# Counting the first signs in 128 columns, and finished rows one a step in two stages

## The chip, the cores and the metric

The kernel runs on one core of a Trainium2 chip. Its engines are TensorE (PE, matrix products and transposes), VectorE (DVE), ScalarE (ACT), GpSimd (POOL) and SyncE (SP, which here only issues transfers). Each works through its own list of instructions and waits for the others by semaphores. The metric is the device time of one execution in microseconds; the lower, the better.

## The reference

Two graph layers follow each other, on 4096 nodes with 512 features. `adj` is a dense 4096 x 4096 matrix in which about one entry in 128 is above zero and the others are zero.

```python
# layer 0
head = (adj > 0) / max(sqrt(number of positive entries in the row), 1e-12)
inc = adj + head
x = layernorm(x + (inc @ x) / rowsum(inc))
# layer 1
A2 = adj + I
dscale = diagonal(A2) ** -0.5
temp = A2 @ x @ W.T
y = relu((dscale[:, None] * A2 * dscale[None, :]) @ temp)
out = layernorm(x + y)
```

So there are three products of a 4096 x 4096 matrix with a 4096 x 512 one, a small product with W, and two layer normalisations over 512 features.

## The kernel before

**Tiling.** Matrices are cut into blocks of 128 rows (`P`); there are 32 of them (`NB`), 16 in each half (`NP`). Large products are done with a scheme of seven products for eight on two by two blocks (Strassen's, in Winograd's form), which is why there are sums and differences of operands (`add_up`, `build`, `sum_b`) and combinations of results (`combine`, `outer`). The adjacency matrix comes three times: transposed in chunks for layer 0 (`adj_q`), natural by rows for counting (`adj`), and transposed in the order of layer 1 (`adj_r`).

**The start.** Layer 0 treats its first pair of row blocks (block 0 of the upper and of the lower half) apart, since nothing has been counted yet. Chunks c = 0 to 3 (`NC`) hold these rows transposed, in an upper half (h = 0) and a lower half (h = 1). SP issues, in this order: the four upper halves (`load_half(0, c)`), the rows of x for steps kk = 0 to 9 (`load_x`, two transfers of 256 KB each), the four lower halves, x for kk = 10 to 15, and then natural rows (`load_natural`, five buffers). `count_half` counts the positive entries of a row: ACT makes signs (+1 or -1) in bfloat16 in one of two `sr` buffers (`signs`, L347), and PE multiplies them by a matrix of ones (L358), which adds over the partitions and leaves the sum on every partition; `idle_products` (L363) are products whose result nobody reads. `scale_half` adds the four blocks of 128 columns that are left (L367, DVE), takes the root (L351, ACT), a lower bound and the reciprocal (L369, L370, DVE). `upper_inc` (L459, L471, L472) then makes the upper half of `inc` out of the chunk, and `multiply_plain(0, c, top)` (L510) multiplies it, four steps kk for each chunk; each step needs x of that kk. The lower half is counted between steps of `multiply_plain(0, 2, top)`; then `to_inc` (L459, L466) makes its `inc` and `multiply_plain(1, c, low)` multiplies it. Between these, DVE makes the operands of the later scheme (`build`, `build_last`) and sums that are stored for layer 1 (`raw_sums`, L440, in the same `sr` buffers, stored by POOL at L449); ACT counts natural rows (`count`, sixteen at a time, L347), each count giving a buffer free for the next natural load on SP. The next chunk (`load_chunk(NC)`, L323) stands behind these on SP. When it is there, `prepare1` readies it, and the large products of layer 0 begin (`multiply1`, L497).

**Layer 1.** `steps` lists two passes: k = 2 (A2 times x, then by W) and k = 3 (A2 times that). Each has two halves of columns s = 0 and 1, in each seven products p, and for each p a group of eight steps kk. For k = 3 the order of p is 2, 3, 5, 1, 6, 7, 4. One step is seven products (`multiply2`, L293), which PE runs as 14 matmuls of 512 columns, into seven banks of PSUM; an eighth bank (`spare`) is for everything else. `prepare` makes the sums of operands two steps ahead (L168, L170, L171, DVE). At the end of a group's last step, kk = 7, `outer` takes the seven banks into C: ACT copies q1 (L712) and q5 (L715), DVE does the rest (`inner`, L713 to L720, with an addition into C, L723 or L727, where p is 6, 7 or 4). The next group starts with the bank of q1.

**Rows that are finished.** After p = 6 the upper half of C is complete for that s, after p = 4 the lower half. Eight row units per half are then put in `queue` (the last half as four pairs, `layer1_first`). A unit, `layer1`, turns 128 rows back by four transposes into the spare bank (`turn_back`, L868), after the step's matmuls, or ahead of the fourth product where a second unit is taken (`between`); ACT scales and rectifies them into one of four buffers `o` (`rectify`, L872). In the next step its `rest` adds the residual y (three buffers, fetched by POOL, L885), takes mean and variance (L150, L152), the root (ACT, L154), the reciprocal (DVE, L160), the normalisation (ACT, L163), and stores (POOL, L901). One unit is taken a step in kk = 1 to 5; in the last two groups two a step in kk = 1 to 6:

```python
end = n >= len(steps) - 2 * NQ
items = [queue.pop(0) for _ in range(min(len(queue), 2 if end else 1))] if 1 <= kk <= (6 if end else 5) else []
```

The order inside a step is the order of the program text: `prepare` of the step after next, `sum_b`, what was `deferred` from `outer`, the products with what stands `between`, the units taken, the `rest` of the step before (`held`), `fetch`, and at kk = 7 `outer`. The last four steps are prepared like the others but multiplied product by product in `finish` (L946), with the last rows.

Of the kernel before, what the change touches and what calls it, by code (L numbers as in the profile page):

```python
# [8 lines left out]
F32 = mybir.dt.float32  # L9
BF16 = mybir.dt.bfloat16  # L10
AF = mybir.ActivationFunctionType
ALU = mybir.AluOpType

P = 128
# [6 lines left out]
B11, B21, B22, T1, T2, T3, T4 = range(7)  # L21
# [5 lines left out]
def tile_adj_resnorm_d2(  # L27
# [37 lines left out]
    nc = tc.nc  # L65
    N, D = x.shape
    H = D // 2
    NB = N // P
    NP = NB // 2
# [38 lines left out]
    nc.gpsimd.memset(tiny, -(2.0 ** -63))  # L108
    half_n = const.tile([P, 1], F32, name="half_n")
    nc.gpsimd.memset(half_n, N / 2)  # L110

    nc.scalar.activation(small.tile([P, 1], F32, name="sd"), eps_t, AF.Sqrt)
    dscale = const.tile([P, NB], F32, name="dscale")
# [231 lines left out]
    def signs(y, a, accum=None):  # L345

        nc.scalar.activation(y, a, AF.Sign, bias=tiny, scale=2.0 ** 64, accum_out=accum)  # L347

    def to_scale(n, total):

        nc.scalar.activation(n, total, AF.Sqrt, bias=half_n, scale=0.5)  # L351

    def count_half(h, c, ps):

        m = w1_pool.tile([P, 2, CW], F32, name="sr", bufs=2).bitcast(BF16)[:, :, 0:CW]
        signs(m, chunks[c][:, 2 * h:2 * h + 2, :])
        for z in range(2):
            nc.tensor.matmul(ps, ones_b, m[:, z, :], start=(c + z == 0), stop=(c == NC - 1 and z == 1))  # L358

    def idle_products(times):  # L360

        for _ in range(times):
            nc.tensor.matmul(bank(2), ones_b, idle, start=True, stop=True)  # L363

    def scale_half(h, ps):
        n = scale[0][:, h, :]
        nc.vector.tensor_reduce(n, ps.rearrange("p (b i) -> p i b", i=P), axis=mybir.AxisListType.X, op=ALU.add)  # L367
        to_scale(n, n)
        nc.vector.tensor_scalar(n, n, EPS, None, op0=ALU.max)  # L369
        nc.vector.reciprocal(n, n)  # L370

# [211 lines left out]
    def load_half(h, c):  # L583
        nc.sync.dma_start(out=chunks[c][:, 2 * h:2 * h + 2, :], in_=adj_q[0, c][:, 2 * h:2 * h + 2, :])
# [5 lines left out]
    nc.gpsimd.memset(feats[-1][:, 1, T2, 0:H], 1.0)  # L590
    idle = feats[-1][:, 1, T2, 0:H].bitcast(BF16)
    for c in range(NC):
        count_half(0, c, ps)
        idle_products((0, 3, 0, 8)[c])
    for kk in range(10):
        load_x(kk)
    for c in range(NC):
        load_half(1, c)
    for kk in range(10, NP):
        load_x(kk)  # L600
    for s in feats:
        nc.gpsimd.memset(s[:, :, B11:B21 + 1, H:W], 1.0)
        nc.gpsimd.memset(s[:, :, T1, H:W], 1.0)
# [12 lines left out]
    build(2)  # L616
    upper_inc(3, slice(0, CW))
    ps = spare()
    multiply_plain(0, 2, top, {i: lambda i=i: [count_half(1, c, ps) for c in (i, i + 1)] for i in (0, 2)})
    build(3)  # L620
    scale_half(1, ps)
    count(16)
    raw_sums(0)
    to_inc(0, 1)
    build(4)
    multiply_plain(0, 3, top)
    top = take(0, top)
    build(5)
    raw_sums(1)
# [92 lines left out]
    def add(o, y):  # L722
        nc.vector.tensor_add(o, o, y)  # L723
# [163 lines left out]
    def layer1(h, item):  # L887

        j, r, cols = item
        b = j + h * NP  # L890
        y = late.pop(b)
        o = late["pool"].tile([P, D], F32, name="o", bufs=4)
        ps = spare()
        turn_back(ps, 0, h, r, cols, (0, 1))
        rectify(o, ps, b)

        def rest():
            add(o, y)
            mv, sd = statistics([o])
            normalise(o, mv, sd)  # L900
            nc.gpsimd.dma_start(out=out[b * P:(b + 1) * P, :], in_=o)  # L901
        later.append(rest)

    def layer1_first(h, *items):


        ps = spare()
        for i, (j, r, cols) in enumerate(items):
            turn_back(ps, i * H, h, r, cols, (1,))
        j, r, _ = items[0]  # L910
        b = j + h * NP
        if ("st", r) not in late:
            late["st", r] = late["pool"].tile([P, 4, 2 + 2 * r, 6], F32, name=f"st{r}")
        st = late["st", r]
        o = late["pool"].tile([P, 2, D], F32, name=f"o{b}")
        nc.scalar.activation(o[:, :, H:D], ps.rearrange("p (i d) -> p i d", i=2), AF.Relu)
        y, late[b] = late[b], (late[b], o)

        def rest():
            for i in range(2):  # L920
                nc.scalar.activation(y[:, i, :], y[:, i, :], AF.Copy, scale=late["root"][:, b + i:b + i + 1])
            add(o[:, :, H:D], y[:, :, H:D])

            w = H // (1 + r)
            for i in range(2):
                for p in range(H // w, D // w):
                    nc.vector.bn_stats(st[:, j % SB + i, p, :], o[:, i, p * w:(p + 1) * w])  # L927
        later.append(rest)

    def finish(h, items, acc):  # L930

# [126 lines left out]
    for n, (k, s, p, kk) in enumerate(steps):  # L1058
# [6 lines left out]
            prepare(n + LA)  # L1065
        if n % 2 == 0 and n // 2 + 1 < len(groups):
            sum_b(n // 2 + 1)
        end = n >= len(steps) - 2 * NQ
        items = [queue.pop(0) for _ in range(min(len(queue), 2 if end else 1))] if 1 <= kk <= (6 if end else 5) else []
        held = later[:]  # L1070
        later.clear()
        while deferred:
# [24 lines left out]
            load_b_up_to(n // 2 + 3)  # L1097
        for item in items:
            take_up(item)
        for rest in held:  # L1100
            rest()
        for pair in going[::-1]:
            next(pair)
        if kk in (4, 6):
            del going[:1]
        if 1 <= kk <= (6 if end else 5):
            for kind, args in queue[:2]:
                fetch(kind, *args)
        if kk == NQ - 1 and n + 1 < len(steps):
# [16 lines left out]
        if n + 1 == len(steps) // 2:  # L1126
# [10 lines left out]
            pools["turn"] = [ring3] * 2 + pools["turn"][i:] + pools["turn"][:i]  # L1137
            made["a"] = 0
            PF = 3
    while later:  # L1140
        later.pop(0)()
    assert not queue
    finish(1, last, acc)

# [31 lines left out]
```

## Time and profile before

| | |
|---|---|
| median of 3 runs | 2277.02 us (2276.03 to 2277.81) |
| the profiled execution, its own time | 2276.97 us |
| span of its instructions | 2275.0 us |
| PE busy | 2252.4 us (99%) |
| DVE busy | 1847.0 us (81%) |
| ACT busy | 538.3 us (24%) |
| POOL busy | 293.3 us (13%) |
| mean granted clock of PE | 0.998 |
| transferred | 564.06 MB, mean 248 GB/s |

In the profile a line such as `L168 DVE TENSOR_TENSOR s<-a` names the line of the kernel, the engine, the operation, and the tile written and read. "PE q L868 <- ACT o L872" in the view of waits says that PE, at line 868, stood idle until ACT had finished line 872. The timeline gives the start, the duration, and in brackets the idle time of the engine before it. PE is busy nearly always, so times when it is idle, or runs at a lower clock, are what an edit can win or lose.

### The profile page before, as it was taken

To read this page: it belongs to the slowest core of one execution; us is meant where nothing else is said; L and a number is where in the kernel's file an instruction comes from. 1 tells how busy PE (TensorE), PEld (TensorE's weight loads), DVE (VectorE), ACT (ScalarE), POOL (GpSimd) and SP (SyncE) were. 2 spreads that over 40 slices of the span, in tenths; PEclk is the share of its full clock that TensorE was granted. 3 is DMA by queue.
4 is the path that set the end of the run, shared out by engine and by line. 5 is a ranking of instruction groups with operands and counts; after the bars stand their busy time and mean duration, and the time that the engine had idled before them with its cause. 6 is when DMAs were issued, how large, how long until landed. Compare 5 with 4: busy or idle time off the path is not lost.

```text
span 2275.0 us, 22101 instructions
## 1 busy us (share of the span) xinstructions
PE 2252.4 (99%) x7360; PEld 1381.4 (61%) x7361; DVE 1847.0 (81%) x2613; ACT 538.3 (24%) x1336; POOL 293.3 (13%) x394
## 2 busy tenths in 40 slices
PE   8999999999999999999999999999999999999998
PEld 6888888888888844444555444555544444444443
DVE  6998998989899887788876887987767788767776
ACT  4336555545553000000111100111110011100022
POOL 0111112211112110002112200112210010000010
PEclk9999999999999999999999999999999999999999
DMA  9778777878776575675677776577775687766673
GB/s 329 269 264 287 253 261 262 272 259 269 250 249 221 186 284 211 218 297 187 249 270 220 236 256 257 189 289 267 220 241 217 236 292 278 261 231 225 235 295 127
DMA packets 168401, 564.06 MB, mean 248 GB/s; under 512 B 17616, under 2 KB 46304, under 8 KB 129888
## 3 DMA queue, kind: packets, MB, share of 16 engines
q1 hardware_dynamic: 120384, 455.13, 56.5%
q0 software_dynamic: 32288, 92.85, 12.8%
q10 hardware_dynamic: 15616, 14.69, 1.9%
q8 instruction: 58, 0.95, 0.2%
q14 instruction: 55, 0.45, 0.1%
HBM read 438.85 MB, written 123.74 MB: 247 GB/s over the span
## 4 chain that ended last, share of the span: by engine, by line
PE 93%; DMA 3%; DVE 2%; issue 1%; ACT 1%; SPq 0%; POOL 0%; ACTq 0%; DVEq 0%; POOLq 0%
PE q L293 56%; PE q L497 32%; PE q L794 4%; DMA b<-x 1%; DMA nat<-adj 1%; DMA a<-adj_q 1%; PE q L946 1%; PE q L868 0%; DMA out<-o 0%; DVE s L168 0%; ACT nat L347 0%; DVE o L723 0%; DVE s L170 0%; DVE st L927 0%; DVE c L723 0%
## 5 line engine op out<-in xcount | busy, mean ns | idle before, releaser
L293 PE MATMUL q<-s,ts 128*128 128x512 f32 x1320 | 609.8, 592 | 0.0
L497 PE MATMUL q<-b,s 128*128 128x256 f32 (+1 forms) x1920 | 453.5, 378 | 1.8 <-DVE s L170 1.8
L293 PEld LDWEIGHTS q<-s,ts 128*128 128x128 f32 x1320 | 250.3, 190 | 295.9 <-issue 269.3
L168 DVE TENSOR_TENSOR s<-a 128x1024 f32<-128x1024 f32 x234 | 290.2, 1240 | 160.2 <-PE q L293 133.2
L497 PEld LDWEIGHTS q<-b,s 128*128 128x128 f32 x1920 | 362.6, 189 | 54.1 <-DVE s L170 2.2
L497 PE MATMUL q<-b,a 128*128 128x256 f32 (+1 forms) x1440 | 350.5, 379 | 0.0
L293 PE MATMUL q<-a,tr 128*128 128x512 f32 x688 | 328.5, 594 | 0.0
L497 PEld LDWEIGHTS q<-b,a 128*128 128x128 f32 x1440 | 272.7, 189 | 38.3
L293 PE MATMUL q<-s,tr 128*128 128x512 f32 x440 | 224.7, 592 | 0.0
L293 PEld LDWEIGHTS q<-a,tr 128*128 128x128 f32 x688 | 129.5, 191 | 143.5 <-issue 137.8
L347 ACT ACTIVATE nat<-nat,tiny 128x512 f32<-128x512 f32 x240 | 172.8, 721 | 33.0 <-DMA nat<-adj 26.8
L293 PE MATMUL q<-a,ts 128*128 128x512 f32 x344 | 175.8, 592 | 0.0
L170 DVE TENSOR_TENSOR s<-a,s 128x512 f32<-128x512 f32 x234 | 166.8, 713 | 8.0
L171 DVE TENSOR_TENSOR s<-a,s 128x512 f32<-128x512 f32 x234 | 164.0, 701 | 8.0
L712 ACT COPY p<-q 128x512 f32<-128x512 f32 x27 | 15.8, 584 | 647.1 <-PE q L293 647.1
L459 DVE SCALAR_TENSOR_TENSOR mask<-a,sc 128x1024 f32<-128x1024 f32 (+2 forms) x129 | 154.2, 1197 | 2.1
L466 DVE TENSOR_TENSOR a<-a,mask 128x1024 f32<-128x1024 f32 x123 | 150.7, 1225 | 6.2
L293 PEld LDWEIGHTS q<-s,tr 128*128 128x128 f32 x440 | 83.6, 190 | 91.6 <-issue 82.7
L395 ACT ACTIVATE nat<-nat 128x512 f32<-128x512 f32 x192 | 118.4, 616 | 18.6 <-DMA nat<-adj 18.6
L293 PEld LDWEIGHTS q<-a,ts 128*128 128x128 f32 x344 | 65.3, 190 | 82.5 <-issue 77.5
L801 POOL TENSOR_TENSOR y<-c,c 128x256 f32<-128x256 f32 x16 | 20.8, 1302 | 639.5 <-DVE c L727 389.9
L449 POOL DMA_DIRECT2D oa<-sr x64 | 57.9, 904 | 282.6 <-DVE sr L440 183.6
(215 smaller groups left out, 2117.9 us busy)
## 6 DMA issues: line engine op xcount, KB each, us to landing
a<-adj_r SPq DMA_DIRECT2D x112, 1024.0 KB, 6.9
a<-oa SPq DMA_DIRECT2D x80, 1024.0 KB, 5.3
nat<-adj SPq DMA_DIRECT2D x240, 256.0 KB, 6.1
a<-adj_q SPq DMA_DIRECT2D x60, 1024.0 KB, 6.2
tr<-ob SPq DMA_DIRECT2D x112, 512.0 KB, 4.0
oa<-sr POOLq DMA_DIRECT2D x64, 512.0 KB, 7.3
oa<-r SPq DMA_DIRECT2D x32, 1024.0 KB, 9.7
y<-x POOLq DMA_DIRECT2D x64, 256.0 KB, 8.1
```

Source lines behind the costliest of these rows:

```text
L168: nc.vector.tensor_add(s[:, S3:S1 + 1, :], a[:, A11:A22 + 1, :], a[:, A21, :].unsqueeze(1).to_broadcast([P, 2, w]))
L170: nc.vector.tensor_add(s[:, S2, :], a[:, A11, :], s[:, S1, :])
L171: nc.vector.tensor_add(s[:, S4, :], a[:, A12, :], s[:, S2, :])
L293: nc.tensor.matmul(acc[m], left, right, start=(kk == 0), stop=(kk == NQ - 1))
L347: nc.scalar.activation(y, a, AF.Sign, bias=tiny, scale=2.0 ** 64, accum_out=accum)
L395: nc.scalar.activation(nat, nat, AF.Copy, accum_out=totals[j][:, h, t:t + 1])
L449: nc.gpsimd.dma_start(out=dst, in_=sr.rearrange("p m (k i) -> p (m k) i", i=P))
L459: nc.vector.scalar_tensor_tensor(m, v, 0.0, s.unsqueeze(1).to_broadcast(list(v.shape)), op0=ALU.is_gt, op1=ALU.mult)
L466: nc.vector.tensor_add(z, z, y)
L497: nc.tensor.matmul(acc[m][:, 0:w], left, b[:, right, 0:w], start=(kk == 0), stop=(kk == NP - 1))
L794: nc.tensor.matmul(ps, left[:, e, :], wt[:, right, e, :], start=(e == 0), stop=(e == 1))
L946: nc.tensor.matmul(acc[m], left, right, start=False, stop=(kk == NQ - 1))
```

## The change

It has two parts that touch no common line.

At the start, the upper half's signs are multiplied by ones in pieces of 128 columns that all add up in the same 128 columns of the bank, so that the reduction on DVE is left out and the root reads the bank. The last chunk's signs are made by two engines: ACT makes one block as before, DVE the other as 2 or 0 instead of +1 or -1, which the constant `half_m` allows for. A copy of one column on POOL, out of the first signs and into the place where x's first rows are loaded, makes the loads of x stand behind the first signs. The last idle products are five instead of eight. The lower half's loads are spread behind x of kk = 8 to 11. The lower half's counts move: chunks 0 and 1 in the third step of the third multiplication, chunks 2 and 3 at the head of the fourth, with `raw_sums(0)` and `build(4)` in front of that and the scale after it.

Towards the end, one row unit is taken in each step with kk of 1 to 7, and two only in the last group. What follows a unit is split in two stages, in the two steps after it: for `layer1` the addition and the statistics first, then root, normalisation and store; for `layer1_first` the scaling on ACT first, then addition and statistics on DVE.

```diff
--- before.py
+++ after.py
@@ -108,6 +108,8 @@
     nc.gpsimd.memset(tiny, -(2.0 ** -63))
     half_n = const.tile([P, 1], F32, name="half_n")
     nc.gpsimd.memset(half_n, N / 2)
+    half_m = const.tile([P, 1], F32, name="half_m")
+    nc.gpsimd.memset(half_m, (N - CW) / 2)
 
     nc.scalar.activation(small.tile([P, 1], F32, name="sd"), eps_t, AF.Sqrt)
     dscale = const.tile([P, NB], F32, name="dscale")
@@ -346,16 +348,26 @@
 
         nc.scalar.activation(y, a, AF.Sign, bias=tiny, scale=2.0 ** 64, accum_out=accum)
 
-    def to_scale(n, total):
-
-        nc.scalar.activation(n, total, AF.Sqrt, bias=half_n, scale=0.5)
+    def to_scale(n, total, half=half_n):
+
+        nc.scalar.activation(n, total, AF.Sqrt, bias=half, scale=0.5)
 
     def count_half(h, c, ps):
 
+
         m = w1_pool.tile([P, 2, CW], F32, name="sr", bufs=2).bitcast(BF16)[:, :, 0:CW]
-        signs(m, chunks[c][:, 2 * h:2 * h + 2, :])
-        for z in range(2):
-            nc.tensor.matmul(ps, ones_b, m[:, z, :], start=(c + z == 0), stop=(c == NC - 1 and z == 1))
+        a = chunks[c][:, 2 * h:2 * h + 2, :]
+        if h == 0 and c == NC - 1:
+
+            signs(m[:, 0, :], a[:, 0, :])
+            nc.vector.tensor_scalar(m[:, 1, :], a[:, 1, :], 0.0, 2.0, op0=ALU.is_gt, op1=ALU.mult)
+        else:
+            signs(m, a)
+        w = CW if h else P
+        parts = [m[:, z, i:i + w] for z in range(2) for i in range(0, CW, w)]
+        for i, y in enumerate(parts):
+            nc.tensor.matmul(ps[:, 0:w], ones_b, y, start=(c == 0 and i == 0), stop=(c == NC - 1 and i == len(parts) - 1))
+        return m
 
     def idle_products(times):
 
@@ -364,8 +376,11 @@
 
     def scale_half(h, ps):
         n = scale[0][:, h, :]
-        nc.vector.tensor_reduce(n, ps.rearrange("p (b i) -> p i b", i=P), axis=mybir.AxisListType.X, op=ALU.add)
-        to_scale(n, n)
+        if h:
+            nc.vector.tensor_reduce(n, ps.rearrange("p (b i) -> p i b", i=P), axis=mybir.AxisListType.X, op=ALU.add)
+            to_scale(n, n)
+        else:
+            to_scale(n, ps[:, 0:P], half_m)
         nc.vector.tensor_scalar(n, n, EPS, None, op0=ALU.max)
         nc.vector.reciprocal(n, n)
 
@@ -590,14 +605,15 @@
     nc.gpsimd.memset(feats[-1][:, 1, T2, 0:H], 1.0)
     idle = feats[-1][:, 1, T2, 0:H].bitcast(BF16)
     for c in range(NC):
-        count_half(0, c, ps)
-        idle_products((0, 3, 0, 8)[c])
-    for kk in range(10):
+        m = count_half(0, c, ps)
+        if c == 0:
+
+            nc.gpsimd.tensor_copy(out=slots[0][:, B11, 0:1], in_=m[:, 0, 0:1])
+        idle_products((0, 3, 0, 5)[c])
+    for kk in range(NP):
         load_x(kk)
-    for c in range(NC):
-        load_half(1, c)
-    for kk in range(10, NP):
-        load_x(kk)
+        if 8 <= kk < 8 + NC:
+            load_half(1, kk - 8)
     for s in feats:
         nc.gpsimd.memset(s[:, :, B11:B21 + 1, H:W], 1.0)
         nc.gpsimd.memset(s[:, :, T1, H:W], 1.0)
@@ -616,14 +632,14 @@
     build(2)
     upper_inc(3, slice(0, CW))
     ps = spare()
-    multiply_plain(0, 2, top, {i: lambda i=i: [count_half(1, c, ps) for c in (i, i + 1)] for i in (0, 2)})
+    multiply_plain(0, 2, top, {2: lambda: [count_half(1, c, ps) for c in (0, 1)]})
     build(3)
+    raw_sums(0)
+    build(4)
+    multiply_plain(0, 3, top, {0: lambda: [count_half(1, c, ps) for c in (2, 3)]})
     scale_half(1, ps)
     count(16)
-    raw_sums(0)
     to_inc(0, 1)
-    build(4)
-    multiply_plain(0, 3, top)
     top = take(0, top)
     build(5)
     raw_sums(1)
@@ -894,12 +910,18 @@
         turn_back(ps, 0, h, r, cols, (0, 1))
         rectify(o, ps, b)
 
+        st, mv, sd = (late["pool"].tile([P, w], F32, name=t, bufs=4) for t, w in (("st", 6), ("mv", 2), ("sd", 1)))
+
+        def measured():
+            add(o, y)
+            nc.vector.bn_stats(st, o)
+            nc.vector.bn_aggr(mv, st)
+
         def rest():
-            add(o, y)
-            mv, sd = statistics([o])
+            nc.scalar.activation(sd, mv[:, 1:2], AF.Sqrt, bias=eps_t)
             normalise(o, mv, sd)
             nc.gpsimd.dma_start(out=out[b * P:(b + 1) * P, :], in_=o)
-        later.append(rest)
+        later.append([measured, rest])
 
     def layer1_first(h, *items):
 
@@ -916,16 +938,18 @@
         nc.scalar.activation(o[:, :, H:D], ps.rearrange("p (i d) -> p i d", i=2), AF.Relu)
         y, late[b] = late[b], (late[b], o)
 
-        def rest():
+        def divided():
             for i in range(2):
                 nc.scalar.activation(y[:, i, :], y[:, i, :], AF.Copy, scale=late["root"][:, b + i:b + i + 1])
+
+        def rest():
             add(o[:, :, H:D], y[:, :, H:D])
 
             w = H // (1 + r)
             for i in range(2):
                 for p in range(H // w, D // w):
                     nc.vector.bn_stats(st[:, j % SB + i, p, :], o[:, i, p * w:(p + 1) * w])
-        later.append(rest)
+        later.append([divided, rest])
 
     def finish(h, items, acc):
 
@@ -1065,8 +1089,8 @@
             prepare(n + LA)
         if n % 2 == 0 and n // 2 + 1 < len(groups):
             sum_b(n // 2 + 1)
-        end = n >= len(steps) - 2 * NQ
-        items = [queue.pop(0) for _ in range(min(len(queue), 2 if end else 1))] if 1 <= kk <= (6 if end else 5) else []
+        end = n >= len(steps) - NQ
+        items = [queue.pop(0) for _ in range(min(len(queue), 2 if end else 1))] if kk else []
         held = later[:]
         later.clear()
         while deferred:
@@ -1097,13 +1121,14 @@
             load_b_up_to(n // 2 + 3)
         for item in items:
             take_up(item)
-        for rest in held:
-            rest()
+        for stages in held:
+            stages.pop(0)()
+        later[:0] = [stages for stages in held if stages]
         for pair in going[::-1]:
             next(pair)
         if kk in (4, 6):
             del going[:1]
-        if 1 <= kk <= (6 if end else 5):
+        if kk:
             for kind, args in queue[:2]:
                 fetch(kind, *args)
         if kk == NQ - 1 and n + 1 < len(steps):
@@ -1137,8 +1162,9 @@
             pools["turn"] = [ring3] * 2 + pools["turn"][i:] + pools["turn"][:i]
             made["a"] = 0
             PF = 3
-    while later:
-        later.pop(0)()
+    for stages in later:
+        for stage in stages:
+            stage()
     assert not queue
     finish(1, last, acc)
 
```

## The prediction

> **What bounds the kernel now.** I read part 1 of the page first: TensorE (PE) is busy for 2252.4 of 2275.0 us, so an edit counts only where PE waits. The view of waits, PE alone, lists all of them:
>
> ```profile
> engine line waited for: us in total, times, longest us
> PE q L358 <- ACT sr L347: 6.6, 3, 6.2
> PE q L868 <- ACT o L872: 3.2, 1, 3.2
> PE q L497 <- DVE s L170: 1.8, 1, 1.8
> PE q L868 <- DVE c L727: 0.9, 1, 0.9
> ```
>
> L358 is the first count, L868 the transposes of finished rows, L497 the first big multiplication. Then the chain, 30 to 80 us, for what ends the 1.8:
>
> ```profile
> 33.70 7.26 DMA nat<-adj
> ...
> 47.14 5.59 DMA nat<-adj
> ...
> 56.54 0.17 DVE n L403
> ...
> 57.34 8.93 DMA a<-adj_q
> ...
> 74.86 0.70 DVE s L170
> 75.56 0.04 issue
> 75.61 4.60 PE q L497 x20
> ```
>
> Not PE leads here but transfers: natural rows, their counts on ACT, and behind these on SP the next chunk, landed at 66.27, with 9.2 us of DVE work after it. PE comes with 1.8 us to spare. Next the clock around the 3.2 us wait (the second last columns are PEclk, DMA share, GB/s at the end):
>
> ```profile
> 2188.00:2192.00 4.00, 0.84 (x2) 0.01 (x1) 2.17 (x4) 0.69 (x1) 0.89 (x2) 0.97 1.05 385
> 2192.00:2196.00 4.00, 3.95 (x9) 2.30 (x10) 1.75 (x5) 1.68 (x3) 0.35 (x1) 0.61 0.72 293
> ```
>
> The wait costs more than its length: afterwards the clock is 0.61. Last the timeline, for one row unit (transposes, L872, L154, L160, L163) and the wait itself:
>
> ```profile
> 2174.80 0.60 PE L868 MATMUL q<-ident,c 128*128 128x128 f32 x4
> 2175.24 1.88 PE L293 MATMUL q<-a,tr 128*128 128x512 f32 x4
> 2175.44 0.69 ACT L872 ACTIVATE o<-q,dscale 128x512 f32<-128x512 f32 x1 [3.19 <-PE q L868]
> 2176.02 0.28 ACT L154 ACTIVATE sd<-mv,eps_t 128x1 f32<-128x1 f32 x1
> 2176.34 0.16 DVE L160 RECIPROCAL rs<-sd 128x1 f32<-128x1 f32 x1 [4.86 <-ACT sd L154]
> 2176.73 0.81 ACT L163 ACTIVATE o<-o,nb,rs 128x512 f32<-128x512 f32 x1 [0.43 <-DVE nb L162]
> ...
> 2191.31 0.69 ACT L872 ACTIVATE o<-q,dscale 128x512 f32<-128x512 f32 x1 [4.34 <-DMA out<-o]
> 2192.05 1.11 PE L868 MATMUL q<-ident,c 128*128 128x128 f32 x4 [3.21 <-ACT o L872]
> ```
>
> A row's rectification waited for a result buffer `o` whose store had not landed; PE's next transposes wait for that bank.
>
> **What the Trainium skill says.** "TensorE: Matmul & The Clock Gate", What's actually happening: the PE clock is halved after an idle window of about 3.4 us and comes back after a busy one; the window runs free. The trace agrees: 3.2 us idle, then 0.61. The same page, Architectural detail: ACT and DVE are strict FIFOs. The trace agrees: L154's input was ready at 2171.48, yet it ran at 2176.02, behind L872. That decides this case.
>
> **The change, first part (start of the kernel).** Removed: the DVE reduction L367 and its hand-over (11.68 to 12.46, 0.78 us), three idle products. Halved: the last signs, 1.15 us on ACT. The nearest row for the DVE half is a 128x512 scalar_tensor_tensor, 0.69; from below the 128x128 tensor_scalar, 0.23; I take 0.6, beside ACT's half: 0.5 saved. Eight matmuls of 128 columns replace two of 512 (0.43 together): between 0.43 and 8 times the 0.11 spacing of L868; I take 0.6: 0.2 lost. First product 1.1 us sooner, at about 14.0. Bounds: 0.8 if the split counts (c = 1 with three idle products) queue up on PE; 2.4 if x, now held back by the small GpSimd copy until the first signs (6.1 us), lets the fourth chunk land sooner (chunks 0 and 1 are 1.3 us apart, later ones more). The copy costs a GpSimd slot like the 0.13 us memsets and delays nothing else: SP's first x issue goes from 2.68 to about 6.4, but its data moved only from about 8, behind the chunks.
>
> The second count: in the built program the signs of chunks 2 and 3 get the same `sr` buffer, as `raw_sums(0)` now takes the other. So chunk 3's signs wait until PE has read chunk 2's, at the head of the fourth multiplication. From the pair in the trace: PE reads at 29.02, ACT starts at 29.70, takes 1.15, PE 0.05 later: 1.88, less the 0.43 of PE's reading: a new PE wait of 1.45 us. The half loads pass behind x rows 8 to 11 on SP; the same bytes go at the same rate (348 GB/s, DMA full), and the last x (issued 32.95, 6 to 7.3 us to land, so by 40.3) is needed at about 42. The store of `raw_sums(0)` moves from 38.7 to about 32 on GpSimd's queue, among the x loads: up to 1.5 us on them, inside that.
> PE so reaches its 1.8 us wait at 73.8 - 1.1 + 1.45 = 74.2. The chain of natural rows and chunk loads holds the same bytes in front of it and ends at 75.6. **Sum of part one: 0** (-2.4 if that chain moves up too; +1.5 if x comes late).
>
> **Second part (rows).** One step is 14 matmuls, 6.01 us, and 0.43 with transposes. In the upper half's last group two units a step made the 3.2; one a step, statistics a step later and the rest another step later, gives each of the four `o` buffers four steps (25 us): removed. Measured from where the next matmul would have run (2188.68) to 2192.05 it is 3.37, and the four transposes and four matmuls after it took 3.71 instead of 2.16: 1.55 of half clock. The 0.9 (L727 before the last group's first transposes) goes too, as an old row stands there now; 0.4 (last operands) is counted below. **Removed: 3.37 + 1.55 + 0.93 + 0.38 = 6.2 us.**
>
> Added, in the built order: units now run in steps 1 to 7 of 8, not 1 to 5. Step 7 ends with `outer`, whose copy (L712, q1 out of its bank) stood free on ACT: it ran at 2207.12, in the middle of step 7, as q1 is finished first. Now ACT's queue reads rectification (7th row), root and normalisation of the 5th row, then this copy. The rectification needs transposes at the *end* of step 7. With Z the start of the next matmul, by the unit above (Z = 2175.24): rectification Z+0.20, root +0.78, DVE reciprocal +1.10, normalisation +1.49 to +2.31, copy (0.59, page) +2.21 to +2.80, PE's first matmul of the next group +2.85. Nothing hides this: PE's queue holds exactly that matmul. DVE first measures the 6th row (0.69 + 0.69 + 0.18, to +3.0), then reads q2 (to 3.64) and q6 (4.36, or 4.96 where `outer` adds into C between); PE wants q6's bank at 4.57 and later q4's: 0.45 + 0.25 more where it adds. Such boundaries: p = 7 in s = 0 (3.55), p = 2 in s = 1 (2.85), p = 7 in s = 1 (3.55): 9.95 us.
>
> In the last group the delay goes on. DVE runs outer (7.8), a prepare (2.7) and L727 (2.3) before the 6th row's reciprocal at Z+15.4; its normalisation ends at 16.6, the 8th row's rectification at 17.2 on ACT behind it, and PE, at 16.0, wants its bank for the next transposes: 1.25. In the last steps root and reciprocal of the 8th row stand behind the last rectification (after step 3's transposes); DVE's prepare of the last step then gives its S2 at 41.1 after Z, PE asks at 40.5: 0.65 in place of 0.38. **Added: 9.95 + 1.25 + 0.65 = 11.85.** Three idle times of 2.7 us: shorter than the 3.2 that dropped the clock, longer than the 1.8 that did not; I take one drop in three, at least one likely, 1.2 us net (DVE catches up meanwhile). Bounds 0 to 4.5.
>
> Sum against the profiled execution's 2276.97 (1.95 around its span): 2276.97 + 0 - 6.2 + 11.85 + 1.2 = **2283.8**; that execution is at the median, 2277.02. I say 2283.5.
>
> **Rivals.** *All three boundaries drop the clock*: +3.3 more, 2287. For it: half clock after 3.2. Against: shorter, and only if the window lies badly. *The start gains in full*: DMA chain 2.4 earlier and no clock lost: 2276.97 - 2.4 + 5.65 = 2280.2, within 0.2%. Against: the chain is all transfers of the same bytes. *Faster: the boundary copy is not held up*, because the 7th row's transposes and rectification still end inside PE's cover; then only the gains remain: 2276.97 - 6.2 + 0.65 = 2271.4. It decides where the new waits sum to under 1.6 us. Against: the copy needs 0.20 + 0.69 + 0.59 after the last transpose even with nothing between. *The change does not do what it says*: the 3.2 stays; then 2288, within the first rival.
>
> **How the numbers follow.** Likeliest 0.55 (own range 2281 to 2286), three drops 0.13, full start 0.20, faster 0.12. A measurement tells 0.2%, 4.6 us, from no change. Faster 0.12; same 0.20 + 0.02; slower 0.53 + 0.13 = 0.66. The range 2277.5 to 2288 leaves out the faster case and the top of the second.
>
> **What would show it.** PE waits: L868 <- ACT o gone; three new waits of about 2.7 us of the group's first L293 on the copy p<-q, with ACT's order rectification, root, normalisation, copy before each; PEclk near 0.6 after some of them; 1.4 us for the count at about 36 us; the wait at 75 us still there, shorter. If the copies stand free in mid step, or the big multiplication starts 2 us sooner, I am wrong.

## The result and the profile after

| | before | after |
|---|---|---|
| median of 8 runs each | 2276.28 us | 2285.64 us |
| lowest and highest | 2275.19 to 2277.81 | 2281.85 to 2288.19 |
| ratio, 95% interval | | 1.0039 [1.0028, 1.0050] |
| profiled execution, own time | 2276.97 | 2288.19 |
| span of its instructions | 2275.0 | 2285.8 |
| mean granted clock of PE | 0.998 | 0.996 |

The changed kernel is slower by 9.4 us in the medians. Its profiled execution is the longest of its eight, 2.5 us above the median, so its waits and clock are those of an execution longer than most.

The waits of PE in the changed kernel (the line that waited, the one that released it, total us, times, longest):

```profile
engine line waited for: us in total, times, longest us
PE q L295 <- ACT p L728: 8.2, 3, 2.7
PE q L369 <- ACT sr L349: 7.8, 3, 6.3
PE q L447 <- DVE d L432: 2.8, 1, 2.8
...
PE q L970 <- DVE c L172: 0.5, 1, 0.5
```

The 3.2 us on `o` and the 0.9 us on `c` are gone. In their place stand three waits of 2.7 us of a group's first matmul (L295) on the copy of q1 (L728). They lie at the boundaries, the changes from one group to the next, that follow groups in which rows are taken. The wait of the big multiplication (1.8 us before) is gone too, but only because PE now comes later: 2.8 us have appeared ahead of it, at L447, the small product that spreads the scale of the next natural rows.

The chain of the changed kernel from 30 to 80 us (start, us, what) shows what L447 waits for:

```profile
35.79 7.01 DMA nat<-adj
...
43.67 2.89 DMA nat<-adj
...
47.48 6.33 DMA nat<-adj
...
54.73 3.98 DMA nat<-adj
...
59.65 0.17 DVE n L418
...
61.04 0.29 DVE d L432
...
61.47 1.19 PE q L447 x2
```

The first natural row lands at 42.80 us (40.96 before), the reduction of the counts runs at 59.65 (L403 at 56.54 before), the scale reaches PE at 61.47 (58.49 before, and there without a wait, as the timeline of before has no bracket behind it):

```profile
58.49 0.59 PE L432 MATMUL q<-d,ones_f 128*128 128x256 f32 x2
```

The timeline of the first of the three boundaries (start, duration, engine, line, operation; in brackets the idle time before it):

```profile
1865.51 0.60 PE L884 MATMUL q<-ident,c 128*128 128x128 f32 x4
...
1866.20 0.69 ACT L888 ACTIVATE o<-q,dscale 128x512 f32<-128x512 f32 x1 [4.34 <-PE q L884]
1866.79 0.28 ACT L921 ACTIVATE sd<-mv,eps_t 128x1 f32<-128x1 f32 x1
1867.10 0.16 DVE L162 RECIPROCAL rs<-sd 128x1 f32<-128x1 f32 x1 [1.44 <-ACT sd L921]
...
1867.50 0.81 ACT L165 ACTIVATE o<-o,nb,rs 128x512 f32<-128x512 f32 x1 [0.43 <-DVE nb L164]
...
1868.22 0.56 ACT L728 COPY p<-q 128x512 f32<-128x512 f32 x1
...
1868.83 1.13 PE L295 MATMUL q<-a,tr 128*128 128x512 f32 x2 [2.72 <-ACT p L728]
```

In the kernel before, the copy at such a place followed nothing but an idle stretch of ACT, in the middle of step 7:

```profile
2207.12 0.59 ACT L712 COPY p<-q 128x512 f32<-128x512 f32 x1 [2.34 <-PE q L293]
```

Here ACT's order is rectification of the seventh row, root and normalisation of the fifth, then the copy. The next matmul would have run at about 1865.95; it runs 2.88 us later. The clock after this wait, and after the one at L447, is in the windows of the changed kernel (length, then busy time of PE, its weight loads, DVE, ACT, POOL, then PEclk, DMA share, GB/s; a PEclk of 0.50 is called half clock below):

```profile
62.00:64.00 2.00, 2.00 (x6) 1.61 (x5) 1.97 (x3) 1.31 (x4) 0.89 (x1) 0.50 0.98 376
...
1866.85:1870.26 3.41, 1.43 (x4) 0.62 (x4) 3.02 (x8) 2.19 (x6) 0.54 (x1) 1.00 1.03 392
1870.26:1873.67 3.41, 3.41 (x5) 1.17 (x4) 3.06 (x6) 0.00 (x0) 0.00 (x0) 0.50 0.29 118
```

In this execution the clock dropped after all three boundaries and after L447. Where the 10.8 us between the two spans arose can be read by taking the start of the same matmul in both timelines; the difference grows or shrinks at these places:

| place | matmul, before and after | difference | step |
|---|---|---|---|
| big multiplication, the matmul that waited before (L497, L512) | 75.61, 78.27 | +2.66 | +2.66 |
| first pass of layer 1, waits for DVE at the W product | 1439.62, 1442.77 | +3.15 | +0.49 |
| after the boundary of p = 7, s = 0 | 1887.33, 1895.17 | +7.84 | +4.69 |
| after the boundary of p = 2, s = 1 | 1986.98, 1999.19 | +12.22 | +4.38 |
| last boundary taken alone (p = 7, s = 1) | 2206.06 to 2214.22 | | +4.69 |
| the waits removed around 2188 and 2221 | 1986.98 to 2222.21 | +10.06 | -6.41 |
| the last steps and the row still to come | to the end | +10.8 | +0.3 |

The two times of the last boundary are those of before; its step is the rise of the difference from 6.06 to 11.18, less 0.43 us, as the changed kernel does a row there that before had already done. In the line after it, the changed kernel at 2222.21 has done one row (0.44 us) less than before. Without that row the remainder would read -6.85; here it is taken off and added to the last line, with the end of the program.

### The profile page after: what moved, and what is told of

Read it like the earlier page. It is cut to its first block, busy times and chain, and to the rows that moved or that the text cites. A ratio compares the mean times of both kernels' runs of the same rounds, so it can differ in the third digit from the quotient of the medians.

```text
span 2285.8 us, 22146 instructions
## 1 busy us (share of the span) xinstructions
PE 2256.3 (99%) x7382; PEld 1384.7 (61%) x7382; DVE 1846.2 (81%) x2613; ACT 536.8 (23%) x1336; POOL 293.5 (13%) x396
## 4 chain that ended last, share of the span: by engine, by line
PE 95%; DMA 2%; DVE 1%; ACT 1%; SPq 0%; issue 0%; POOL 0%; ACTq 0%; DVEq 0%
PE q L295 57%; PE q L512 32%; PE q L810 4%; DMA b<-x 1%; DMA nat<-adj 1%; PE q L525 1%; PE q L970 1%; PE q L884 1%; DMA a<-adj_r 0%; DVE r L254 0%; DMA a<-adj_q 0%; SPq L333 0%; ACT nat L349 0%; SPq L332 0%; ACT o L165 0%
## 5 line engine op out<-in xcount | busy, mean ns | idle before, releaser
L295 PE MATMUL q<-s,ts 128*128 128x512 f32 x1320 | 610.9, 593 | 0.0
L512 PE MATMUL q<-b,s 128*128 128x256 f32 (+1 forms) x1920 | 453.4, 378 | 0.0
L295 PEld LDWEIGHTS q<-s,ts 128*128 128x128 f32 x1320 | 251.4, 191 | 300.0 <-issue 270.5
L170 DVE TENSOR_TENSOR s<-a 128x1024 f32<-128x1024 f32 x234 | 289.9, 1239 | 169.5 <-PE q L295 145.2
L512 PEld LDWEIGHTS q<-b,s 128*128 128x128 f32 x1920 | 362.7, 189 | 52.0
L512 PE MATMUL q<-b,a 128*128 128x256 f32 (+1 forms) x1440 | 350.5, 379 | 0.0
L295 PE MATMUL q<-a,tr 128*128 128x512 f32 x688 | 331.0, 598 | 8.2 <-ACT p L728 8.2
L512 PEld LDWEIGHTS q<-b,a 128*128 128x128 f32 x1440 | 272.7, 189 | 38.3
L295 PE MATMUL q<-s,tr 128*128 128x512 f32 x440 | 224.7, 592 | 0.0
L295 PEld LDWEIGHTS q<-a,tr 128*128 128x128 f32 x688 | 129.4, 191 | 151.4 <-issue 135.1
L295 PE MATMUL q<-a,ts 128*128 128x512 f32 x344 | 175.7, 592 | 0.0
L172 DVE TENSOR_TENSOR s<-a,s 128x512 f32<-128x512 f32 x234 | 166.7, 713 | 8.0
L728 ACT COPY p<-q 128x512 f32<-128x512 f32 x27 | 15.8, 584 | 660.2 <-PE q L295 660.2
L295 PEld LDWEIGHTS q<-s,tr 128*128 128x128 f32 x440 | 83.6, 190 | 91.6 <-issue 83.7
L295 PEld LDWEIGHTS q<-a,ts 128*128 128x128 f32 x344 | 65.4, 190 | 82.3 <-issue 77.5
```

The lines of the kernel that those rows point to most:

```text
L170: nc.vector.tensor_add(s[:, S3:S1 + 1, :], a[:, A11:A22 + 1, :], a[:, A21, :].unsqueeze(1).to_broadcast([P, 2, w]))
L172: nc.vector.tensor_add(s[:, S2, :], a[:, A11, :], s[:, S1, :])
L295: nc.tensor.matmul(acc[m], left, right, start=(kk == 0), stop=(kk == NQ - 1))
L512: nc.tensor.matmul(acc[m][:, 0:w], left, b[:, right, 0:w], start=(kk == 0), stop=(kk == NP - 1))
```

## The experiments

Ratios are against the kernel before on the same chip; 0.001 is 2.3 us.

### Which part costs

**start_only** and **rows_only**: the kernel before with only the first part of the diff (down to the scale of the second count), and with only the second.

> The first part of the change alone on the kernel before. Theory: the start loses by itself. Its store of raw sums now goes ahead of the last x rows, natural rows land 1.8 us later, their count ends 3 us later, and PE waits about 2.8 us at L447 for the scale (operand d) and loses about 1 us more at half clock; it enters the big multiplication 2.7 us later than before: 2279 us. Rival, the sum of the prediction: the start is worth nothing (the big multiplication starts at the same time, 75.6 us), 2276.3 us, and all the loss is in the rows.

Measured 1.0009 [1.0001, 1.0018]: +2.0 us.

> The second part of the change alone on the kernel before. Theory: three waits of 2.7 us at the first matmul of a group, each followed by half clock (1.9 us more), against 4.9 + 0.9 us removed: 2282.5 to 2283 us. Rival: whether the clock drops hangs on where the idle time lies against a window; here everything lies 3 us earlier, so one to three of the drops can be missing: 2281 with two drops, 2279 with one, 2277 with none, the three waits of 2.7 us unchanged.

Measured 1.0031 [1.0019, 1.0042]: +7.1 us. The two add up to 9.1 of the 9.4 us. So the start does not come out at nothing, and the rows cost about what they were said to, with an interval of 4.3 to 9.6 us. In the waits of PE of rows_only the same three stand (its numbers of lines are those of before), and one more, of the last group:

```profile
PE q L293 <- ACT p L712: 8.1, 3, 2.7
...
PE q L868 <- ACT o L872: 1.0, 1, 1.0
```

The windows after its three boundaries, with columns as above, show that its rival was right about the clock:

```profile
1864.00:1868.00 4.00, 3.70 (x8) 1.49 (x9) 3.62 (x8) 0.75 (x3) 0.44 (x1) 1.00 0.68 279
...
1967.00:1971.00 4.00, 3.52 (x6) 1.64 (x7) 3.65 (x7) 1.10 (x3) 0.55 (x1) 0.73 0.64 264
...
2216.00:2220.00 4.00, 3.83 (x9) 1.51 (x10) 3.65 (x7) 0.63 (x2) 1.38 (x3) 1.00 0.98 348
```

Equal waits of 2.7 us, one drop in three here, three in three in the changed kernel's profile. Its six runs went from 2281.8 to 2288.4 us, a spread in which differing numbers of drops would fit; only the profiled runs show the clock by place, so that is not shown for the others.

### What makes the boundary wait

**copy_first**: ACT's copy of q1 ahead of the rows in step 7, DVE's order left.

```diff
+        if k == 3 and kk == NQ - 1 and n + 1 < len(steps):
+            copied.append(copy_of(acc[0]))
         for item in items:
             take_up(item)
```

(`inner` then takes `copied.pop()` in place of its own copy.)

> The changed kernel, with ACT's copy of q1 (layer 1, second pass) issued ahead of what the rows issue in step 7; DVE's order is unchanged. Theory that the wait is not ACT's alone: the copy now runs in mid step 7, but DVE measures the sixth row before it reads q2, up to 3.6 us after the step's end, while PE now wants q2's bank 0.9 us after it: three waits of about 2.7 us for DVE instead of ACT, with about the same clock loss, 2284 to 2286 us. Rival, that ACT's queue order is the whole cause: the three waits and drops go, 14 us less, 2271.5 us.

Measured 1.0033 [1.0020, 1.0045], +7.5 us; its profile's PE waits, and the timeline of the first boundary:

```profile
PE q L295 <- DVE y L736: 5.3, 2, 2.7
PE q L295 <- DVE c L736: 2.7, 1, 2.7
```

```profile
1861.43 1.02 PE L295 MATMUL q<-a,tr 128*128 128x512 f32 x2
...
1863.59 0.70 DVE L924 BATCH_NORM_STATS2 st<-o 128x6 f32<-128x512 f32 x1
...
1864.41 0.66 DVE L736 TENSOR_TENSOR y<-q,p 128x512 f32<-128x512 f32 x1
...
1865.13 1.13 PE L295 MATMUL q<-a,tr 128*128 128x512 f32 x2 [2.67 <-DVE y L736]
```

Two matmuls of the new group now run at once, and the third waits 2.67 us for q2's bank, which DVE reads only after the sixth row's statistics. The theory held: the wait is as long on DVE as on ACT, and freeing one queue gains nothing that the runs show. Its ratio is that of the changed kernel (1.0039) within both intervals.

**outer_first**: the whole of `outer` ahead of the rows in step 7, for both engines.

```diff
+        if k == 3 and kk == NQ - 1 and n + 1 < len(steps):
+            outer(k, p, acc)
         for item in items:
             take_up(item)
```

(and it is left out at its old place for k = 3.)

> The changed kernel, units in steps 1 to 7, but in layer 1's second pass the whole of outer (both copies on ACT and all of DVE's work) stands ahead of the row units in step 7. Theory: with both engines' queues put right, ACT's copy and DVE's reads, the three waits and the drops go, which moving ACT's copy alone did not reach: 2273 to 2275 us, the rows only come later. Rival: DVE's 7.8 us of outer now delay the fifth to seventh rows' reciprocals, ACT stands at their normalisation, and the next unit's rectification holds up PE's spare bank: waits of 2 us or more at L884 in each of the next groups, 2279 us or more.

Measured 0.9999 [0.9991, 1.0007]: 9 us under the changed kernel by the ratios. No wait of L295 is left in its PE waits, and the rival's wait comes once:

```profile
PE q L884 <- ACT o L888: 2.6, 1, 2.6
```

It stands in the last group, where the eighth row's rectification is behind the sixth row's normalisation, which DVE's `outer` has delayed; half clock follows it. Both readings were partly right: 9 us come from the order of two queues, and part of the delay comes back later.

**six**: units in steps 1 to 6 (`if 1 <= kk <= 6`), the rest as changed. **rows_six** is the same without the first part.

> The changed kernel with units taken in steps 1 to 6 instead of 1 to 7; the eighth step of a group takes none. Theory: the waits come from what the seventh unit puts ahead of outer in step 7 (on ACT its rectification, on DVE the measure of the sixth row), so without it the three waits at the first matmul of a group and their drops of the clock go; the sixth row's measure now ends in mid step 7. The gains of the rows stay (6.2 us less than before), the start keeps its 2 us: 2273 us. Rival: root and normalisation of the fifth row still stand ahead of the copy in step 7 and hold it up; waits of 1 to 2 us stay at each boundary, 2277 to 2280 us.

> The kernel before with the second part of the change only, and units in steps 1 to 6. Theory: no loss at the boundaries, the o wait of 3.2 us with its 1.5 us of half clock and the 0.9 us gone: 6 us less than before, 2270.5 us, and 2 us less than the same rows with the new start. Rival: the rows' gain hangs on the start (DVE-bound stretches give part of it back), 2273 to 2275 us.

Measured 1.0014 [1.0007, 1.0021], +3.2 us, and 1.0005 [0.9997, 1.0013], +1.1 us. Here my theory fell, and for six the rival held: three waits on L728 are left, 3.8 us in all, the longest 1.6. In rows_six, where the same waits sum to 4.2, neither guess reached the time. The timelines of ACT and of DVE in six, around the first boundary:

```profile
1860.63 0.29 ACT L921 ACTIVATE sd<-mv,eps_t 128x1 f32<-128x1 f32 x1 [0.74 <-DVE mv L918]
1863.99 0.81 ACT L165 ACTIVATE o<-o,nb,rs 128x512 f32<-128x512 f32 x1 [3.06 <-DVE nb L164]
1864.71 0.56 ACT L728 COPY p<-q 128x512 f32<-128x512 f32 x1
```

```profile
1861.01 1.23 DVE L170 TENSOR_TENSOR s<-a 128x1024 f32<-128x1024 f32 x1
1862.27 0.69 DVE L172 TENSOR_TENSOR s<-a,s 128x512 f32<-128x512 f32 x1
1863.00 0.69 DVE L173 TENSOR_TENSOR s<-a,s 128x512 f32<-128x512 f32 x1
1863.61 0.15 DVE L162 RECIPROCAL rs<-sd 128x1 f32<-128x1 f32 x1
```

The root was there at 1860.9, but DVE does the next operands before the reciprocal; ACT stands 3.06 us at the normalisation, with the copy behind it. "Mid step" was too early a guess: here DVE does the `prepare` that stands first in a step before it comes to the step's rows. With two stages a unit of step 5 or 6 leaves its normalisation or its measure in step 7; the stages themselves carry rows into the boundary. The other place named in six's waits, 1.0 us at L884 in the last group, is the one of rows_only.

**rows_four**: units in steps 1 to 4, the largest number that leaves nothing in step 7; on the start of before.

> The kernel before with the second part of the change only, and units in steps 1 to 4. With two stages a unit's normalisation comes two steps after it, so this is the largest number that leaves nothing of a row in step 7. Theory: the 1.6 us waits that stayed with six steps are the fifth row's normalisation in step 7, behind DVE's prepare; here the three boundary waits are gone, and of the waits removed (3.37 + 1.55 of half clock + 0.93) nothing is given back: 2270.5 us. Rival: what was won in the last groups is lost to something else in the last group, where eight units now have to go two a step (a wait at L868 on o or on the spare bank): 2273 to 2276 us.

Measured 0.9997 [0.9989, 1.0005]: the boundary waits are gone, as the theory said, and so is the gain, as the rival said. PE's waits in the last groups:

```profile
PE q L868 <- ACT o L922: 3.4, 2, 2.7
PE q L958 <- DVE c L1006: 1.3, 1, 1.3
```

At 2222 us, by the same matmul, it was 7.6 us ahead of the kernel before, or 5.9 without the four rows that it had still to do; at the end 1.2.

### What the start loses

**store_late** (the changed kernel) and **start_late** (the kernel before with the first part): `raw_sums(0)` back behind `count(16)`. **moves_only**: the kernel before with nothing but the moved second count, `raw_sums(0)` and `build(4)`.

```diff
     build(3)
-    raw_sums(0)
     build(4)
     multiply_plain(0, 3, top, {0: lambda: [count_half(1, c, ps) for c in (2, 3)]})
     scale_half(1, ps)
     count(16)
+    raw_sums(0)
     to_inc(0, 1)
```

> The changed kernel, with raw_sums(0) back behind the natural counts, so that its store is issued late as before and the four second counts have two buffers in turn again. Theory that the early store delays the natural rows: they land near 41 us again, the wait at L447 shrinks from 2.8 to about 1.2 us without a drop of the clock, the 1.3 us wait for the count goes, and the big multiplication starts near 75.6 us: 2.7 us less than the changed kernel, 2283 us. Rival, that the small GpSimd copy, which holds back the loads of x, delays the natural rows: they land at 42.5 us as in the changed kernel, PE waits over 4 us at L447, 2285.6 us.

> The kernel before with the first part of the change only, but raw_sums(0) and its store at their old place behind the natural counts. Theory: the early store is what costs; the natural rows land 1 to 1.5 us earlier than with the whole first part, the wait at L447 for the scale stays at most 1.5 us, and the time is that of before, 2276.5 us. Rival: the loads of x, held back by the GpSimd copy, are what costs: 2278.5 us as with the whole first part, and the first natural row lands no earlier than 41.6 us.

> The kernel before with only the moves at the start: second counts later, raw_sums(0) and build(4) in front of the fourth multiplication. Loads, counting columns and the split signs are those of before. Theory: the early store of raw_sums(0) delays the natural rows by itself: the first lands at 41.6 to 42.8 us instead of 40.4 to 41.0, the scale comes 1 to 3 us later, PE, which also waits 1.3 us for the count, reaches L432 near 59.8 us and waits up to 1.5 us; 1 to 2 us slower than before, 2277.5 to 2278.5 us. Rival: only together with the held-back loads of x does it matter; the first natural row lands by 41 us and the time is 2276.5 us.

Measured: store_late 1.0039 [1.0027, 1.0052], no gain over the changed kernel in five runs, though its one profile had the waits that were expected (1.5 us at L447, none for the count, the big multiplication at 74.3 us); start_late 1.0003 [0.9995, 1.0012]; moves_only 1.0005 [0.9999, 1.0012]. The times do not part the theories: the intervals of start_only, start_late and moves_only lie over each other. What the traces say is clearer. First natural row in start_only and in start_late, from the chains (start and duration of the transfer):

```profile
34.85 7.06 DMA nat<-adj
```

```profile
34.86 5.86 DMA nat<-adj
```

Issued at the same moment, it lands 1.2 us earlier where the store comes late. Over all profiles it landed at 41.6 to 42.8 us in the five with the first part as changed (after, start_only, copy_first, six, outer_first), at 40.7 in the two with the late store, at 40.4 to 41.0 in the six with the start of before. So the store's place goes with when the first natural rows land, and the GpSimd copy, which is in all seven, does not by itself make them late. But the later rows come late all the same (the sixteenth at 55.9 and 57.3 us with the late store, 55.3 to 56.5 with the start of before, 56.5 to 58.7 as changed), and PE then waits at L447: 1.5 and 2.9 us. moves_only turned out to be no test of an early store: with the old order of loads its store was issued at 38.09 us, hardly before the 38.70 of the kernel before, against 33.7 to 34.5 with the first part as changed. Its first natural row landed at 41.15, the fifth at 45.07 (43.6 before). PE was late there for another reason too: its first products started at 17.05 us (15.07 before) and at half clock, and it came to L432 4.3 us later than before, so its waits say little.

A wait at L447 stands in six of the seven profiles with the new start (0.6 to 2.9 us) and once in the six with the old one (1.0 us). The seventh is start_only's own:

```profile
PE q L884 <- ACT o L888: 3.7, 1, 3.7
...
PE q L512 <- DVE s L172: 0.4, 1, 0.4
```

It comes to the big multiplication 0.4 us earlier than before and is still 0.6 us ahead at the start of layer 1's second pass (1547 us in before). It loses 1.4 us at the wait on `o` instead: 3.7 us where before had 3.2, and half clock for 6.8 us instead of 3.4. So L447 is a place where the new start can lose time, not shown to be the place of the 2.0 us. What delays the later natural rows stays open, and so does how much of the 2.0 us each edit of the first part has.

### A version that is faster

**one_a_step**: the kernel before with one edit.

```diff
-        end = n >= len(steps) - 2 * NQ
+        end = n >= len(steps) - NQ
```

> The kernel before with one edit: two units a step only in the last group instead of the last two. Units stay in steps 1 to 5 (6 in the last group) and in one stage. Theory: taking one a step is all that the gain needs, the two stages only bring a row into step 7: the o wait with its half clock and the 0.9 us go, no boundary wait comes, 2270.5 us. Rival: the fourth buffer still comes free too late without the stages, or the last group's two units a step now meet the o wait: 2274 to 2277 us.

**rows_outer**: outer_first without the first part.

> The kernel before with the second part of the change only, units in steps 1 to 7, and outer ahead of the rows in step 7 of layer 1's second pass. Theory: no wait at the three boundaries, but the one of 2.6 us at L868 in the last group (the eighth row's rectification behind the sixth row's normalisation, which waits for DVE's outer, prepare and L727) stays, with half clock of 1.7 us where the window falls so: 6.2 gained, 2.6 to 4.3 given back, 2273 to 2274.5 us. Rival: with the other start the DVE comes earlier and this wait is short: 2271 us.

Measured 0.9989 [0.9982, 0.9995] and 0.9991 [0.9984, 0.9997]: 2.5 and 2.0 us faster than the kernel before, both faster than the changed one. The theory of one_a_step held for the mechanism and not for the size. The wait on `o` at L872 is gone without any stages, and by the same matmul at 2222 us it is 7.7 us ahead of the kernel before, or 6.4 without the three rows that it has still to do. The rows that are no longer done in the last group but one fall into the last, and its waits of PE there are

```profile
PE q L946 <- DVE c L170: 2.6, 1, 2.6
PE q L868 <- ACT o L916: 0.7, 1, 0.7
```

L946 are the last steps; their operands (L170) are behind the additions and statistics of the last rows on DVE, where the kernel before had 0.38 us. In rows_outer it is the wait of 2.8 us at L868 that takes most back, as expected.

## Why the prediction was right where it was

The forecast was 2283.5 us, the measured median 2285.64. Its two sums did not do equally well.

- **Rows, added.** Right: rectification, root, reciprocal, normalisation, copy, next matmul were to end at 2.85 us after the step, and did at 2.88 (in the timeline of the changed kernel). The Trainium skill, "TensorE: Matmul & The Clock Gate", Architectural detail (ACT and DVE strict first in, first out) is borne out by the bracket of 3.06 us in six: a copy whose input was ready stood behind a waiting normalisation. That DVE alone would hold PE as long was in the working (q2 read at 3.64) and copy_first shows it.
- **The 0.45 and 0.25 us more at two boundaries** came where the clock did not drop: those two boundaries cost rows_only 3.54 and 3.71 us by the same matmuls, where 3.55 was said. With a drop they cost 4.6 and 4.7 us in after, 1.0 more, which is less than the 1.7 us that 3.41 us at half clock alone take: PE asks later, so the two costs don't add.
- **Half clock.** Mis-sized in its chance: one drop in three was taken. In after all three came, the first rival's case; over after, rows_only, copy_first and store_late, whose boundary waits are all 2.67 to 2.72 us, 7 of 12 did. The price of a drop, 1.2 us net, was near: 1.0 us at the boundaries above, and at the one after p = 2, said to cost 2.85 us without a drop, 4.4 to 4.7 us with one in these four profiles.
- **Rows, removed.** 3.37 + 1.55 + 0.93 = 5.85 us were said; the step in the table is 6.4. Of the difference, 0.4 is that two rows in a step had cost the kernel before a little besides, over four steps, read from the same matmuls, and 0.2 lies at the second wait.
- **Last group.** The 1.25 us at the transposes is absent in after, whose half clock gives DVE the time, and 1.0 in rows_only, six, rows_six and store_late, where the clock did not drop at the last boundary. The 0.65 for the last operands was 0.52.
- **The rows' sum** of 6.9 us is nearer to the 7.1 measured than its terms deserve: more drops of the clock than were taken, a removal 0.6 larger than was said, and a term of the last group that vanishes with a drop partly cancel. In the profile of rows_only, which had the one drop that was taken, the rows come to 6.8 us by the same matmuls, from the start of the second pass to the end.
- **The start.** Its sum of 0 was wrong: 2.0 us [0.2, 4.1] were lost. 2.0 lies outside the bounds of -2.4 to +1.5; the interval reaches into them. Single terms were near: first product at 13.68 (14.0 said), the wait for the count 1.28 (1.45). In the profile of after, the step that failed is "PE so reaches its 1.8 us wait at 73.8 - 1.1 + 1.45 = 74.2": it came there at 78.27. The sum has no term for the scale of the natural rows, on which PE waited 2.76 us at L447, with half clock behind it. The other step, that the chain of transfers "ends at 75.6", was off by less: what the big multiplication waits for (s, L172) was ready at 76.4. The prediction had moved the store of `raw_sums(0)` among the x loads, 1.5 us, and found that x had room for it, but it did not look at the natural rows behind x on SP. The skill's page "DMA: Bandwidth & Descriptors", Queues, rings and completion order, says that each DMA engine takes turns between the queues with work for it; no view here shows these turns, but it fits that the first natural rows on SP's queue landed 1.2 us later where a store on GpSimd's queue was issued 6 us earlier (start_only against start_late). And the place was not on the list of waits: L432, with its scale ready 0.3 us before PE came, waited for nothing before and so did not appear.
- **Faster**, that the copy is not held up in step 7, was excluded rightly; the numbers that excluded it (0.20 + 0.69 + 0.59 after the last transpose) are near those of the timeline.
- **What would show it.** The new waits, ACT's order, the clock and the count were there as named. "The wait at 75 us still there, shorter" was not, in this profile, as PE had been held up at L447; in start_only it was there with 0.4 us.

So rows 7.1 against 6.9 said (11.85 + 1.2 - 6.2), start 2.0 against 0: by the medians most of the miss of 2.1 us is the start. The intervals, 4.3 to 9.6 and 0.2 to 4.1, leave other splits open.

## What to carry to other kernels

Splitting a row's work into stages moves its last stage to later steps; count in which step each stage lands, on every engine's queue, before spreading the units over more steps, and keep the step that hands PSUM over free of them or behind the hand-over. A list of waits shows what is late, not what is only just in time: before work is moved ahead in a queue, look at the slack of everything that is queued behind it. And a gain in the last but one group is worth only what the last group, with nothing behind it to cover it, does not give back: in one_a_step's profile 6.4 us became 3.3.

## What the runs showed of the hardware

After the first 30 us, an idle time of PE of 2.60 to 2.76 us was followed by half clock in 11 of 18 cases in the fourteen profiles. What decides between equal waits can be read from the traces. In each of them the moments at which the granted clock changes lie whole multiples of 3.413 us apart: in after, the drops at 61.20, 1870.26, 1972.66 and 2221.83 us are 530, 30 and 73 such lengths from one another, and half clock lasted one length, or two where the first still held 1.2 and 1.6 us of idle time (moves_only, start_only). So the clock changes at the edges of windows that the program does not shift. The window 1866.85:1870.26 of after, shown above, is cut at such edges: 1.98 us of it are idle, and the next one is at half clock. (The wait of 3.2 us in the kernel before put 2.89 us into one window.) In rows_only an edge splits the wait of 2.71 us at the first boundary:

```profile
1859.58:1862.99 3.41, 1.83 (x8) 0.82 (x6) 1.90 (x5) 1.07 (x3) 0.00 (x0) 1.00 0.92 317
1862.99:1866.41 3.42, 2.11 (x5) 0.75 (x6) 3.21 (x7) 1.76 (x4) 0.54 (x1) 1.00 1.01 408
1866.41:1869.82 3.41, 3.41 (x8) 1.31 (x8) 3.17 (x5) 0.00 (x0) 0.00 (x0) 1.00 0.14 50
```

Neither of the first two windows holds enough idle time (1.58 and 1.31 us), and the clock stays. With all fourteen traces cut in this way, 15 of the 16 drops after the first 30 us (the end of the program left out) follow a window with 1.97 to 2.89 us of idle time, one follows 1.85, and no window at full clock without a drop behind it has more than 1.95. An estimate from this: an edge saves a wait of 2.72 us only if it lies between about 0.76 and 1.96 us into it, which is 1.2 of 3.4 us, so about two such waits in three drop the clock.

The skill's "TensorE: Matmul & The Clock Gate", What's actually happening, has the halving after an idle window of about 3.4 us that runs free. The length and the free running agree with these traces; that the window must be idle all through does not, since about 2 us of it were enough.

The same start does not take the same time twice. The matmul of the big multiplication that waits in before came at 73.9 to 76.1 us in the six profiles with the start of before, and at 74.6 to 78.3 in the five with the new one. One profile of such a stretch is a sample: the changed kernel came there 2.66 us later than before and start_only 0.4 us earlier, and these two have the same code up to that place.
